# Layer 2: the last nine groups take all their chunks from GpSimd's gathers

## The chip, the core and the metric

The kernel runs on one core of one Trainium2 chip. The core has TensorE (PE, matrix products), VectorE (DVE), ScalarE (ACT) and GpSimd (POOL), each with an instruction stream of its own, and SyncE (SP), which issues DMAs. They wait for one another through semaphores. The metric is the time of one execution on the device in microseconds; lower is better.

## The reference

A graph network of two layers on 12,500 nodes with 128 features and 200,000 edges, sorted by destination:

```python
h = relu(layernorm(x))
w = edge_weight / max(segment_sum(edge_weight, dst), EPS)[dst]
feat = relu(h @ W_pool + b_pool)
neigh = segment_max(feat[src] * w[:, None], dst)
rst = h @ W1_self + neigh @ W1_neigh + b1
h1 = relu(rst / max(norm(rst), EPS))
neigh2 = segment_sum(h1[src] * w[:, None], dst) / max(deg, 1)
out = x + relu(h1 @ W2_self + neigh2 @ W2_neigh + b2)
```

Nearly all the time goes into `feat[src]` and `h1[src]`: for each of the 200,000 edges one row of 128 numbers is fetched from a table of nodes.

## The kernel before

The edges are cut into 391 groups (`NG`) of 512, the last one of 320. A group has four chunks (`j` = 0 to 3) of 128 edges. Layer 1 ends, and layer 2 begins, a little past the middle of the execution; only layer 2 (from line 1134) is of interest here.

Group `g` needs the rows of the table for its 512 sources in a buffer with edges on the partitions. The eight buffers are a ring, `ring[g % 8]`, so group `g` can be filled only after the product of group `g - 8` has read the buffer. A chunk is fetched in one of two ways:

- GpSimd gathers it with one indirect DMA (`gather`, line 513): 128 rows of 512 bytes from the table `h_d` in device memory, one to each partition. The gathers of group `i` are issued at loop step `i`, but GpSimd runs ahead as far as the ring lets it.
- VectorE or ScalarE copies it by columns. The table also lies turned in SBUF (`other_way`: features on partitions, nodes along the free dimension), so one node is one column. ScalarE copies one column per instruction (`one_by_one`, line 792; 128 instructions a chunk), VectorE two (`two_by_two`, line 799; 64 a chunk). Each column's place is a register, loaded sixteen at a time (`places_of`, line 743) from a list that SyncE fetches (`load`, line 738). The chunk stands turned when it is full; TensorE transposes it into PSUM (`turned`, line 1152) and ScalarE writes it back to the buffer (`back`, line 1155).

Which chunks go by columns is set by the class `Columns` (line 711). In layer 2 VectorE takes chunk 1 of every third group from group 17 on, ScalarE chunk 2 of every third or fourth (3.5 on average) from group 12 on. The planner puts a chunk's eight bursts of sixteen columns into the loop steps from `g - 6` on, the transposition into step `g - 2` and the turn back into step `g`. `takes(g)` says whether the group is in the plan; `gather` skips such a chunk.

The loop (line 1218) writes out the order of each engine by hand. A step `i` holds: the gathers of group `i`; on VectorE the placement weights `s` of group `i` (`weighted_places`, line 1164: two instructions, three buffers); node transforms that are due (`nodes2`, line 903); on TensorE the product of group `i - 1` (`window_product`, line 1173: a clearing matmul, line 1177, and eight passes, line 1179, that sum the weighted rows of the edges into 48 destination columns in PSUM, with three accumulators `pa`); on VectorE the addition of group `i - 2` into the sums (`window_add`, line 1181); and column copies in between on VectorE and ScalarE. Every engine works its stream in order: a product that waits for one chunk holds all later products.

The end of the plan is the argument `end` of `Columns`: groups below it can be taken.

Of the kernel before, what the change touches and what calls it, by code (L numbers as in the profile page):

```python
# [43 lines left out]
HIGH = 1.0e30  # L44
KEPT = 4
PAIR = 2


@with_exitstack
def gnn_kernel(ctx, tc, x, src, dst, ew, w_pool, b_pool, w1s, w1n, b1, w2s, w2n, b2, out):  # L50
# [20 lines left out]
    NG = GF + 1  # L71
# [62 lines left out]
    def buffer(g, wide):  # L134
        if not wide:
            return ring[g % RING]
        if WIDE <= g < WIDE + 3:
            k = g - WIDE
            return (work(f"f{k}").rearrange("p (q d) -> p q d", d=D) if k < 2 else ewT[:, 1])
        h = g if g < WIDE else g - 3  # L140
        if h < LESS:
            return ring[h % WIDE]
        return mid[(h - LESS) % MID] if h < LEAST else ring[(h - LEAST) % RING]
# [463 lines left out]
    for i in range(len(groups) + 4):  # L607
# [57 lines left out]
        while raw_chunks and 1 <= i <= 15:  # L665
            r, j = raw_chunks[0]
# [119 lines left out]
    def lists_of(k):  # L786
        return [listed[at:at + 1, :] for at in (64 * k, 64 * k + 32)]

    def by_scalar(out, in_, **scale):
        nc.scalar.activation(out, in_, AF.Copy, **scale)  # L790
# [23 lines left out]
    def wide1(t):  # L814
        return PAIR if t < HI - LATE else 1

# [107 lines left out]
    with tc.manual_schedule(), tc.tile_pool(name="ew", bufs=3) as wk, \  # L924
# [15 lines left out]
        for k, engine, copy, j, every, first in (  # L940
# [6 lines left out]
            def slot(g, k=k, rows_of_chunk=rows_of_chunk):  # L947
                return rows_of_chunk(g) if k else picked[:, bycol[0].place[g], :]
# [185 lines left out]
    with tc.manual_schedule(), tc.tile_pool(name="ew2", bufs=3) as wk, \  # L1134
# [10 lines left out]
        for k, engine, copy, j, every, first in (  # L1145
                (0, mybir.EngineType.DVE, two_by_two, 1, 3, 17),
                (1, mybir.EngineType.Activation, one_by_one, 2, 3.5, 12)):

            def slot(g, j=j):
                return buffer(g, False)[:, j, :]  # L1150

            def turned(g, _, k=k, slot=slot):
                nc.tensor.transpose(flip[:, k], slot(g), ident)  # L1153

            def back(g, _, k=k, slot=slot):
                by_scalar(slot(g), flip[:, k], **({} if k else {"scale": signs}))

            bycol.append(Columns(engine, copy, None, other_way, 1, lists_of(k), slot,
                                 ((-2, turned), (0, back)), 3, j, every, first, NG - 1))
            bycol[k].turned, bycol[k].back = turned, back  # L1160
        nc.vector.memset(agg2, 0.0)
        ss, pas, xrs = ({} for _ in range(3))
# [196 lines left out]
def build(inputs):  # L1359
    import numpy as np  # L1360
    import concourse.bacc as bacc

    nc = bacc.Bacc("TRN2", target_bir_lowering=False, num_devices=1)
    arrays, args = {}, []
    for name in _INS:
        a = np.ascontiguousarray(inputs[name])
        arrays[f"in_{name}"] = a
        args.append(nc.dram_tensor(f"in_{name}", a.shape, mybir.dt.from_np(a.dtype),
                                   kind="ExternalInput").ap())
    args.append(nc.dram_tensor("out", inputs["x"].shape, F32, kind="ExternalOutput").ap())  # L1370
    with tile.TileContext(nc) as tc:
        gnn_kernel(tc, *args)
    return nc, arrays
# [7 lines left out]
```

## Time and profile before

| what | us |
|---|---|
| median of 3 runs | 5087.21 |
| lowest and highest run | 5079.45, 5088.45 |
| profiled execution | 5084.55 |
| span of the profiled execution, first to last instruction | 5082.8 |
| PE, DVE, ACT, POOL busy | 2223.8, 3212.2, 3309.8, 2622.4 |

In rows of a timeline the first number is the start in microseconds from the beginning of the span, the second the time from the first start to the last end of the instructions that the row merges (`x8`: eight of them). Then come engine, line, operation, `out<-in` and shapes; the brackets give the idle time of the engine before the row and what ended it. `gt` is a buffer of the ring, `way` the turned table or the sums, `pa` an accumulator, `flip` the PSUM tile of the transpositions. "issue" means that nothing in the profile ended the wait, "remote" that it was something outside the profile. In the chain of waits a row is a start, a duration and what the time went to, along the work that ended last. In rows of groups a row gives the number of instructions, their busy time, the mean in nanoseconds, and the idle time before them.

### The profile page before, as it was taken

The page shows a single profiled execution, that of the slowest core. Times are in us where ns is not written, and L with a number is a line of the kernel's source. Part 1 is how long each engine was busy: PE and PEld are TensorE (multiplying, and loading weights), DVE is VectorE, ACT ScalarE, POOL GpSimd, SP SyncE. Part 2 cuts the span into 40 slices and gives each one's busy share as a digit, 9 for nine tenths or more (in the row PEclk, how much of TensorE's full clock was granted, in tenths as well). Part 3 has the DMA queues.
Part 4 walks back from the last instruction along what each step waited for, and adds up shares of the span by engine and source line. Part 5 has one row for each costly group of instructions (what it writes and reads, how often), then busy time and mean ns, then how long its engine had stood idle before and what let it go on. Part 6 is the DMA issues. An engine that isn't in the chain of part 4 may idle for free.

```text
span 5082.8 us, 71968 instructions
## 1 busy us (share of the span) xinstructions
PE 2223.8 (44%) x9504; PEld 1947.8 (38%) x9504; DVE 3212.2 (63%) x16738; ACT 3309.8 (65%) x25632; POOL 2622.4 (52%) x2784
## 2 busy tenths in 40 slices
PE   5554445444444444444433444343443334334344
PEld 3344444444444434343333444333333333333334
DVE  4667767676676667666645666565555555655655
ACT  3467767677777767667636666666666666666665
POOL 4454554555555555555554555545544454554453
PEclk6655555555555555555555555555555555555555
DMA  4322222222222222222211111111111111111111
GB/s 151 105 69 59 63 62 59 64 61 62 62 62 63 62 61 63 62 63 62 62 51 35 37 50 46 40 40 40 43 40 41 40 41 40 42 41 39 42 43 36
DMA packets 132987, 280.13 MB, mean 55 GB/s; under 512 B 49446, under 2 KB 58764, under 8 KB 132494
## 3 DMA queue, kind: packets, MB, share of 16 engines
q0 software_dynamic: 88544, 181.42, 14.2%
q1 hardware_dynamic: 43214, 93.11, 5.4%
q14 instruction: 414, 3.39, 0.2%
q8 instruction: 79, 1.29, 0.1%
q10 hardware_dynamic: 736, 0.92, 0.1%
HBM read 253.41 MB, written 21.87 MB: 54 GB/s over the span
## 4 chain that ended last, share of the span: by engine, by line
ACT 50%; issue 33%; POOL 6%; PE 3%; ACTq 3%; DVE 2%; another core or an unknown queue 2%; DMA 1%; DVEq 0%; POOLq 0%
ACT gt L790 35%; ACT gs L1037 8%; POOL gt L520 5%; ACTq L744 3%; ACT rows L1052 2%; PE pa L1179 1%; ACT w2T L790 1%; ACT way L987 1%; ACT locT L790 1%; ACT sq L871 1%; DMA gt<-h_d,srcT 1%; PE pf L624 0%; DVE gt L802 0%; DMA gt<-feat_d,srcT 0%
## 5 line engine op out<-in xcount | busy, mean ns | idle before, releaser
L790 ACT ACTIVATE gt<-way 128x1 f32 x21376 | 2355.0, 190 | 1429.0 <-issue 1379.9
L520 POOL DMA_INDIRECT gt<-h_d,srcT x1318 | 1247.7, 947 | 1202.1 <-PE pa L1179 653.0
L520 POOL DMA_INDIRECT gt<-feat_d,srcT x1192 | 1128.4, 947 | 955.7 <-ACT rows L1052 454.4
L802 DVE SCALAR_TENSOR_TENSOR gt<-b,way 128x2 f32<-128x2 f32 x8000 | 1191.5, 216 | 582.4 <-issue 444.6
L1179 PE MATMUL pa<-s,gt 128*128 128x24 f32 x3102 | 760.2, 390 | 1032.9 <-ACT gt L790 767.0
L1179 PEld LDWEIGHTS pa<-s,gt 128*128 128x128 f32 x3102 | 699.6, 326 | 1115.7 <-ACT gt L790 777.5
L1057 DVE TENSOR_TENSOR_SCAN pm<-kt,carry,pm 128x512 f32<-128x512 bf16 x389 | 498.2, 1281 | 326.1 <-PE pm L1042 261.6
L1042 PE MATMUL pm<-ident,gs 128*128 128x128 f32 x1499 | 405.0, 425 | 604.6 <-ACT gs L1037 559.9
L802 DVE SCALAR_TENSOR_TENSOR picked<-b,way 128x2 f32<-128x2 f32 x3840 | 545.1, 213 | 24.1 <-issue 23.0
L1042 PEld LDWEIGHTS pm<-ident,gs 128*128 128x128 f32 x1499 | 286.3, 224 | 648.3 <-ACT gs L1037 603.0
L1037 ACT ACTIVATE gs<-gt,ewT 128x128 f32<-128x128 f32 x1303 | 417.8, 390 | 47.9 <-issue 38.4
L1106 PEld LDWEIGHTS pn<-sel,rows 128*128 128x128 f32 x1564 | 363.2, 320 | 208.8 <-ACT way L892 97.7
L1106 PE MATMUL pn<-sel,rows 128*128 128x48 f32 x1564 | 362.2, 379 | 177.7 <-ACT way L892 89.3
L1182 DVE TENSOR_TENSOR way<-pa,way 128x48 f32 x391 | 78.9, 202 | 274.2 <-PE pa L1179 122.5
L1069 DVE TENSOR_SCALAR sel<-cols,lastT,invT 128x48 f32<-128x48 f32 x782 | 246.9, 316 | 5.2 <-remote 5.1
L1153 PE MATMUL flip<-ident,gt 128*128 128x128 f32 x233 | 98.5, 455 | 343.2 <-ACT gt L790 313.0
L1097 PE MATMUL pr<-ident,sc 128*128 128x128 f32 x782 | 241.3, 411 | 16.1 <-issue 7.4
L1080 DVE COPY sc<-pm 128x256 f32<-128x256 f32 x391 | 161.7, 414 | 87.9 <-remote 54.0
L1153 PEld LDWEIGHTS flip<-ident,gt 128*128 128x128 f32 x233 | 62.8, 287 | 351.8 <-ACT gt L790 321.2
L1083 DVE COPY_PREDICATED sc<-kt,pm 128x256 f32<-128x256 int16 x389 | 168.6, 433 | 17.8 <-DVE sel L1069 10.9
L1097 PEld LDWEIGHTS pr<-ident,sc 128*128 128x128 f32 x782 | 168.0, 224 | 17.7 <-issue 16.0
L520 POOL DMA_INDIRECT w2T<-feat_d,srcT x96 | 91.3, 951 | 136.4 <-DVE raw_off L543 56.4
(303 smaller groups left out, 2801.5 us busy)
## 6 DMA issues: line engine op xcount, KB each, us to landing
kt<-keep_d SPq DMA_DIRECT2D x97, 512.0 KB
gt<-h_d,srcT POOLq DMA_INDIRECT x1318
gt<-feat_d,srcT POOLq DMA_INDIRECT x1192
feat_d<-fr SPq DMA_DIRECT2D x24, 256.0 KB
xr<-in_x SPq DMA_DIRECT2D x24, 256.0 KB
out<-o SPq DMA_DIRECT2D x24, 256.0 KB
h_d<-h SPq DMA_DIRECT2D x47, 128.0 KB
listed<-at_d SPq DMA_DIRECT2D x359, 0.5 KB
```

The lines of the kernel that those rows point to most:

```text
L520: nc.gpsimd.indirect_dma_start(out=gt[:k, j, :], out_offset=None, in_=table_d[:, :], in_offset=bass.IndirectOffsetOnAxis(ap=srcT[:k, t, j, ...
L790: nc.scalar.activation(out, in_, AF.Copy, **scale)
L802: nc.vector.scalar_tensor_tensor(slot[:, r + e:r + e + 2], zero_high, columns_read[e], columns_read[e + 1].to_broadcast([P, 2]), op0=OP.su ...
L1037: nc.scalar.activation(gss[i][:k, j, :], gt[:k, j, :], AF.Copy, scale=ewT[:k, t, j, r:r + 1])
L1042: nc.tensor.transpose(pms[i - 1][:, j * P:j * P + k], gs[:k, j, :], ident[:k, :k])
L1057: nc.vector.tensor_tensor_scan(pm[:, :ne], kt[:, :ne], pm[:, :ne], carry, op0=OP.add, op1=OP.max)
L1069: nc.vector.tensor_scalar(part, cols[:k, 1, :], lastT[:k, t, j, r:r + 1], invT[:k, t, j, r:r + 1], op0=OP.is_equal, op1=OP.mult)
L1080: nc.vector.tensor_copy(sc[:, :ne // 2], two[:, :, 1])
L1083: nc.vector.copy_predicated(sc[:, :ne // 2], new[:, :, 1], two[:, :, 0])
L1097: nc.tensor.transpose(prs[g][:k, j, :], sc[:, j * P:j * P + k], ident)
L1106: nc.tensor.matmul(pas[g], rows[:k, j, :], sel[:k, j, :], start=j == 0, stop=j == len(chunks) - 1)
L1179: nc.tensor.matmul(pas[g][:, SHIFT[j]:SHIFT[j] + CW], gt[:k, j, :], s[:k, j, :], start=False, stop=j == 0)
```

## The change

The plan of both engines in layer 2 ends at group `NG - 9` = 382 rather than at `NG - 1` = 390. VectorE's chunks of groups 383, 386 and 389 and ScalarE's of groups 383 and 386 leave the plan, with their list loads, register loads, copies, transpositions and turns back. GpSimd gathers these five chunks. Layer 1 keeps its plan.

```diff
@@ -44,6 +44,7 @@
 HIGH = 1.0e30
 KEPT = 4
 PAIR = 2
+CATCH = 9
 
 
 @with_exitstack
@@ -1156,7 +1157,7 @@
                 by_scalar(slot(g), flip[:, k], **({} if k else {"scale": signs}))
 
             bycol.append(Columns(engine, copy, None, other_way, 1, lists_of(k), slot,
-                                 ((-2, turned), (0, back)), 3, j, every, first, NG - 1))
+                                 ((-2, turned), (0, back)), 3, j, every, first, NG - CATCH))
             bycol[k].turned, bycol[k].back = turned, back
         nc.vector.memset(agg2, 0.0)
         ss, pas, xrs = ({} for _ in range(3))
```

## The prediction

> **What bounds the kernel now.** I read the page first, then the chain of waits over the last 40 us, then the timelines of ScalarE, GpSimd and TensorE there, and last the opening of layer 2, the one place where gathers run with few column copies beside them.
>
> ```profile
> span 5082.8 us, 71968 instructions
> ...
> ACT 50%; issue 33%; POOL 6%; PE 3%; ACTq 3%; DVE 2%; another core or an unknown queue 2%; DMA 1%; DVEq 0%; POOLq 0%
> ```
>
> ScalarE and the issue time around it hold most of the chain over the whole span. The change touches only the end, so the end decides:
>
> ```profile
> 5052.71 1.07 ACT gt L790 x8
> 5053.79 0.04 issue
> 5053.83 1.48 PE pa L1179 x6
> ...
> 5061.74 0.28 PE flip L1153
> ...
> 5071.13 1.52 PE pa L1179 x6
> ```
>
> Until 5053.8 the chain runs on ScalarE's column copies; from there it is TensorE alone, product after product. The timeline of TensorE, with the groups counted back from the last product (the only one of 64 rows, group 390):
>
> ```profile
> 5004.86 1.90 PE L1179 MATMUL pa<-s,gt 128*128 128x24 f32 x8
> ...
> 5053.83 1.48 PE L1179 MATMUL pa<-s,gt 128*128 128x24 f32 x6 [7.74 <-ACT gt L790]
> ...
> 5055.88 1.90 PE L1179 MATMUL pa<-s,gt 128*128 128x24 f32 x8
> 5057.71 0.22 PE L1177 MATMUL pa<-nothing,ones_r 1*128 1x48 bf16 x1
> 5057.86 1.90 PE L1179 MATMUL pa<-s,gt 128*128 128x24 f32 x8
> ...
> 5071.06 1.59 PE L1179 MATMUL pa<-s,gt 64*128 64x24 f32 x6
> ```
>
> These are groups 376, 383 (its last six matmuls), 384, 385 and 390. Group 383 waits 7.74 us for ScalarE; then 384 to 389 run back to back, 1.98 us a product with the node transforms between, and 390 starts at 5071.06. The span ends 11.74 us later; that remainder (product, node transforms, stores) is not touched.
>
> ScalarE, which TensorE waited for:
>
> ```profile
> 5002.62 0.25 ACT L790 ACTIVATE gt<-flip 128x128 f32<-128x128 f32 x1
> ...
> 5043.40 0.20 ACT L790 ACTIVATE gt<-way 128x1 f32 x1 [0.50 <-issue]
> 5044.11 9.25 ACT L790 ACTIVATE gt<-way 128x1 f32 x92 [0.51 <-issue]
> 5053.27 0.35 ACT L790 ACTIVATE gt<-flip,b 128x128 f32<-128x128 f32 x1
> ```
>
> The copy at 5002.62 turns back group 376's chunk, and the sixteen copies before it were the last of group 379's. All single columns between 5002.86 and 5053.27 belong to groups 383 and 386. They go at two paces: 92 in 9.25 us, 0.1 us each, and one in 0.7 us (5043.40 to 5044.11). GpSimd's timeline tells them apart:
>
> ```profile
> 5005.15 0.95 POOL L520 DMA_INDIRECT gt<-h_d,srcT  x1 [0.30 <-PE pn L853]
> 5006.41 0.94 POOL L520 DMA_INDIRECT gt<-h_d,srcT  x1 [0.30 <-issue]
> 5009.13 0.95 POOL L520 DMA_INDIRECT gt<-h_d,srcT  x1 [1.78 <-remote]
> ...
> 5040.98 0.95 POOL L520 DMA_INDIRECT gt<-h_d,srcT  x1 [0.30 <-issue]
> 5045.95 0.95 POOL L520 DMA_INDIRECT gt<-h_d,srcT  x1 [4.02 <-issue]
> 5047.20 0.94 POOL L520 DMA_INDIRECT gt<-h_d,srcT  x1 [0.30 <-issue]
> ```
>
> The two at 5005 and 5006 are group 383's, 5009.13 opens group 384, 5040.98 ends 389, and 5045.95 opens 390's three, which end the queue. Gathers stand 1.25 us apart (5045.95, 5047.20). The slow pace of ScalarE ended at 5044.11, three microseconds after the run of gathers that ended at 5040.98. The three late gathers slowed nothing: the 92 copies ran through them. So a long run of gathers slows the other engines, and does so to their messages too: product 376 was through at 5006.76 by its row, and the gather that needs its buffer (376 and 384 share one of eight) started only at 5009.13. I call such a stretch a jam.
>
> **The change part by part.** Chunks 383, 386 and 389 of VectorE and 383 and 386 of ScalarE become gathers.
>
> Removed on ScalarE: 2 x 128 = 256 column copies. The groups between 5002 and 5054:
>
> ```profile
> L790 ACT ACTIVATE gt<-way 128x1 f32 x264 | 29.5, 190 | 21.3 <-issue 21.1
> L802 DVE SCALAR_TENSOR_TENSOR gt<-b,way 128x2 f32<-128x2 f32 x191 | 28.8, 216 | 13.7 <-issue 12.9 <-remote 0.4
> ```
>
> That is 29.5 us of work and 21.3 us of waiting beside it, nearly all of ScalarE's stretch up to 5053.27. ScalarE drops out of the tail; what is late next is either a gather or TensorE. On VectorE 3 x 64 = 192 instructions go, 28.8 us with 13.7 of idle. Those are covered today: 389's chunk is wanted only by a product after 5064, so I take 0 to 1 us for them, and count the gain that they let the weights of the next groups out sooner as nothing. Five list loads on SyncE and their register loads go too; nothing waits behind them at the end, 0. Five transposes and five turns back go; one transpose, 0.28 us in the chain at 5061.74, lies on the path that I keep, so 0.3 us is gained there.
>
> Added on GpSimd: five gathers, 5 x 1.25 = 6.25 us of its queue, two for 383, two for 386, one for 389. How they land: in the opening of layer 2 a product starts as the last gather of its group has landed,
>
> ```profile
> 2613.76 0.95 POOL L520 DMA_INDIRECT gt<-h_d,srcT  x1 [0.31 <-issue]
> ```
> ```profile
> 2608.55 1.90 PE L1179 MATMUL pa<-s,gt 128*128 128x24 f32 x8 [13.35 <-DVE place L1167]
> ...
> 2616.41 1.87 PE L1179 MATMUL pa<-s,gt 128*128 128x24 f32 x8 [2.97 <-DMA gt<-h_d,srcT]
> ...
> 2663.72 1.90 PE L1179 MATMUL pa<-s,gt 128*128 128x24 f32 x8
> ```
>
> so 2616.41 - 2613.76 = 2.65 us from a gather's start to its use.
>
> Now the replay. GpSimd: 383's four gathers run at 5005.15, 5006.41, 5007.66, 5008.91. The jam lasts as long after the run as before, so 384 follows after the same stop, 5009.13 - 5006.41 = 2.72 us, at 5011.63. Each later group waits for the product eight groups earlier. The trace does not show how many products get through in a jam without column copies. Between none and all, I take stops at 386 and 390: eight gathers (384, 385) from 5011.63 to 5020.38, stop, sixteen (386 to 389) from 5023.10 to 5041.85, stop, 390's three from 5044.57, the last at 5047.07, usable at 5049.72. One stop more or less is 2.72 - 1.25 = 1.5 us.
>
> TensorE: 390's first gather needs product 382 to be done and known. TensorE has three accumulators, so it can run at most two products beyond what VectorE could add; I take both, 383 and 384, as done by 5044.57, since nothing of ScalarE holds them any more. Left are 385 to 389, which took 5071.06 - 5057.86 = 13.20 us, less the 0.28 of the transpose. Product 390 starts at 5044.57 + 12.92 = 5057.49, well after its gathers. Against 5071.06 that is **13.6 us**. If only 382 is done, two products of 1.98 us come on top and 9.6 us remain; with one stop more, 8. With two products more and one stop less it is 19. These are the ends for this case.
>
> A rule against the jam: the Trainium skill, "SBUF — State Buffer", section "Who interferes with whom", says that a DMA never contends with a compute engine and that only the port pair shared by VectorE and GpSimd does. The rows here disagree for whatever reason: ScalarE's copies went from 0.1 to 0.7 us apart during the gathers. By the rule the new gathers would delay no engine, which is the third rival's price.
>
> **The rivals.** *The gathers eat it.* The stops of before stay as they are and the five gathers are only added: 390 opens at 5045.95 + 6.25 = 5052.20, product 382 is barely known then, and 383 to 389 follow in 13.20 + 2 x 1.98 = 17.16 us; 390 starts at 5069.4, a gain of 1.7 us, 5085.5 in the terms of the median. For it: GpSimd had stops that were not ScalarE's doing. Against it: the long idle before 5028 and 5045 went with groups that ScalarE and VectorE held.
>
> *The jam starves TensorE: slower.* With ever more gathers in a row the jam need not end. In the opening of layer 2, where gathers ran without a stop, products 3 to 9 took 2663.72 - 2608.55 = 55.17 us, 9.2 each, and VectorE stood still:
>
> ```profile
> 2630.26 0.21 DVE L1182 TENSOR_TENSOR way<-pa,way 128x48 f32 x1 [18.48 <-remote]
> ```
>
> At that pace products 376 to 382 end at 5004.86 + 7 x 9.2 = 5069.3, and 390 starts 17.16 us later, at 5086.4: 15.4 us slower, 5102.6. It decides from 7.0 us a product on ((5071.06 - 17.16 - 5004.86) / 7). Against it: at the opening GpSimd had eight empty buffers, and here each group waits for a product, which ends the run and lets the messages through.
>
> *TensorE keeps up.* With no column copies beside them the gathers slow nothing; 390 starts when its rows land, at 5049.72 with my stops (21.3 us gained, 5065.9), without any stop at 5005.15 + 30 x 1.25 + 2.65 = 5045.3 (25.8 us, 5061.4). For it: three gathers at 5045.95 slowed nothing. Against it: the opening, where VectorE had little to do and still stood for 18 us.
>
> **How the numbers follow.** The profiled execution took 5084.55 us, of which 5082.8 is the span; it lies 2.66 us below the median 5087.21. Less 13.6 it is 5071.0, in terms of the median 5073.6, rounded to 5074. Chances: forecast 0.55, gathers eat it 0.16, starved 0.12, keeps up 0.17. The forecast's own range is a gain of 8 to 19 us, 5068 to 5079. The range for the time reaches from inside the case that keeps up, 5064, to past the eaten one, 5086; outside are the starved case and the fastest end, together under 0.2. A measurement of this kernel tells about 0.2% from no change, 10.2 us. Of the forecast's 0.55 some 0.07 falls short of that. Faster: 0.48 + 0.17 = 0.65; within: 0.07 + 0.16 = 0.23; slower 0.12.
>
> **What would show it.** Right: no single-column copy of ScalarE after about 5003 (counted from the unchanged start of the tail, 80 us before the end); GpSimd in longer runs with stops of some 2.7 us; the first gather of 390 near 5044.6; TensorE's last product near 5057.5, with no wait for ScalarE among the last ten. The added gathers are right if they stand 1.25 us apart. Wrong: product 390 waiting for a gather (then TensorE keeps up), TensorE with waits of 5 us and more between products 376 and 382 (then it starves), or 390's gathers after 5050 (eaten). What would make it wrong above all is the number of products that pass in a jam, which I took as two beyond the last one known.

## The result, and the profile after

| kernel | median of runs, us | lowest, highest |
|---|---|---|
| before, 12 runs on the same chip | 5088.59 | 5079.45, 5097.99 |
| changed, 12 runs | 5083.87 | 5073.76, 5087.32 |
| ratio | 0.9985 | 0.9976 to 0.9994 |

The change gained 7.6 us by the ratio (0.15% of 5088.59; 3.1 to 12.2 by the interval), below the 0.2% that I called telling from no change. The ratio goes by all runs; the two medians lie only 4.7 us apart. The time lies within the stated range of 5064 to 5086, but the gain is just under the 8 us at which the forecast's own range began, and the forecast gain of 13.6 us lies just above the interval.

The tail can be measured more sharply than the total, since executions of one kernel already differ by up to 8 us when the tail begins. From the start of product 375, which the change does not reach, to the start of product 390:

| execution | 375 starts | 390 starts | tail, us |
|---|---|---|---|
| before, first profile | 5001.16 | 5071.06 | 69.9 |
| before, again (e5) | 5001.77 | 5071.24 | 69.5 |
| changed, first profile | 5000.29 | 5061.10 | 60.8 |
| changed, again (e6) | 5008.17 | 5069.00 | 60.8 |
| predicted | 5001.16 | 5057.49 | 56.3 |

The starts of product 375 in the two profiles of the kernel before and in e6 are these rows of TensorE's timeline; those of the changed kernel's first profile stand below.

```profile
5001.16 1.90 PE L1179 MATMUL pa<-s,gt 128*128 128x24 f32 x8
```
```profile
5001.77 1.90 PE L1179 MATMUL pa<-s,gt 128*128 128x24 f32 x8
```
```profile
5008.17 1.90 PE L1180 MATMUL pa<-s,gt 128*128 128x24 f32 x8
```

So 8.7 to 9.1 us came out of the tail, and 4.5 us of the forecast did not. Lines of the changed kernel stand one lower than before (L790 is L791, L1179 is L1180). Its page first, then its chain of waits, then the timeline of TensorE:

```profile
span 5073.8 us, 71452 instructions
...
ACT 51%; issue 31%; DVE 4%; ACTq 4%; PE 3%; POOL 3%; another core or an unknown queue 3%; DMA 1%; DVEq 0%; SPq 0%; POOLq 0%
...
L791 ACT ACTIVATE gt<-way 128x1 f32 x21120 | 2329.3, 191 | 1400.5 <-issue 1379.9
```
```profile
5018.88 5.91 another core or an unknown queue
...
5025.31 16.30 another core or an unknown queue
...
5042.13 7.30 another core or an unknown queue
5049.43 0.20 DVE way L1183
...
5050.15 1.90 PE pa L1180 x8
```
```profile
5000.29 1.90 PE L1180 MATMUL pa<-s,gt 128*128 128x24 f32 x8
...
5006.26 1.90 PE L1180 MATMUL pa<-s,gt 128*128 128x24 f32 x8
...
5017.58 1.90 PE L1180 MATMUL pa<-s,gt 128*128 128x24 f32 x8
...
5019.56 1.90 PE L1180 MATMUL pa<-s,gt 128*128 128x24 f32 x8
...
5025.53 1.90 PE L1180 MATMUL pa<-s,gt 128*128 128x24 f32 x8 [0.27 <-DVE s L1172]
...
5042.36 1.90 PE L1180 MATMUL pa<-s,gt 128*128 128x24 f32 x8 [0.28 <-DVE s L1172]
...
5050.15 1.90 PE L1180 MATMUL pa<-s,gt 128*128 128x24 f32 x8 [0.27 <-DVE s L1172]
...
5061.10 1.59 PE L1180 MATMUL pa<-s,gt 64*128 64x24 f32 x6
```

The products are 375, 377, 382, 383, 384, 385, 386 and 390. ScalarE is gone from the end of the chain, where "another core or an unknown queue" stands instead: a wait whose release the profile cannot name. Products 377 to 383 start 2.2 us apart. Then 384 to 386 take 30.6 us (5019.56 to 5050.15), 10.2 each, and 386 to 390 follow freely in 10.95. The timelines of GpSimd and VectorE show what stood there:

```profile
5008.05 0.94 POOL L521 DMA_INDIRECT gt<-h_d,srcT  x1 [0.30 <-issue]
5011.15 0.94 POOL L521 DMA_INDIRECT gt<-h_d,srcT  x1 [2.17 <-PE pa L1180]
...
5039.92 0.94 POOL L521 DMA_INDIRECT gt<-h_d,srcT  x1 [0.30 <-issue]
5041.87 0.94 POOL L521 DMA_INDIRECT gt<-h_d,srcT  x1 [1.01 <-remote]
...
5044.37 0.91 POOL L521 DMA_INDIRECT gt<-h_d,srcT  x1 [0.30 <-issue]
```
```profile
5024.81 0.21 DVE L1183 TENSOR_TENSOR way<-pa,way 128x48 f32 x1 [5.76 <-remote]
...
5041.63 0.21 DVE L1183 TENSOR_TENSOR way<-pa,way 128x48 f32 x1 [16.15 <-remote]
...
5049.42 0.21 DVE L1183 TENSOR_TENSOR way<-pa,way 128x48 f32 x1 [7.11 <-remote]
```

GpSimd issued all 24 gathers of 384 to 389 in one run, 1.25 us apart, and 390's three after a gap of 1.95. VectorE's three rows are the additions of products 381, 382 and 383, counted back from the last. Product 382 was through at 5017.58 + 1.90 = 5019.48, and VectorE could add it only at 5041.63, 22.2 us later; product 385 needs the accumulator that this addition frees.

The trace also records each update of a semaphore. A product posts five to TensorE's semaphore: one with the clearing matmul and one with every second pass. Those of the changed kernel from 5020 on, in us:

```
5020.53  5022.66  5024.78 | 5026.89  5029.01  5032.51  5036.71  5041.61 |
5045.11  5047.94  5048.65  5049.35  5049.40 | 5049.43  5049.47  5049.52 ...
```

At each bar the fifth update of a product is in, and VectorE's addition follows 0.02 to 0.03 us later (5024.81, 5041.63, 5049.42). The updates come out one at a time, at distances that are multiples of 0.70 to 0.71 us (2.12, 3.50, 4.20, 4.90), though TensorE finished all of 381 to 383 by 5021.5. After 5049.35 the rest comes out 0.04 us apart. So for TensorE the jam is a backlog of messages. ScalarE's single copies of before had the same distance (5043.40 to 5044.11), but the profile does not name what they waited for.

### The profile page after: what moved, and what is told of

It is laid out like the page before. It is cut to its first block, busy times and chain, and to the rows that moved or that the text cites. A ratio compares the mean times of both kernels' runs of the same rounds, so it can differ in the third digit from the quotient of the medians.

```text
span 5073.8 us, 71452 instructions
## 1 busy us (share of the span) xinstructions
PE 2221.2 (44%) x9499; PEld 1946.7 (38%) x9499; DVE 3185.5 (63%) x16546; ACT 3283.6 (65%) x25371; POOL 2627.5 (52%) x2789
## 4 chain that ended last, share of the span: by engine, by line
ACT 51%; issue 31%; DVE 4%; ACTq 4%; PE 3%; POOL 3%; another core or an unknown queue 3%; DMA 1%; DVEq 0%; SPq 0%; POOLq 0%
ACT gt L791 37%; ACT gs L1038 8%; ACTq L745 3%; POOL gt L521 3%; ACT rows L1053 2%; PE pa L1180 1%; DVE gt L803 1%; ACT way L988 1%; ACT w2T L791 1%; ACT locT L791 1%; ACT sq L872 1%; DMA gt<-feat_d,srcT 1%; DVE pm L1058 0%; ACT gt L957 0%
## 5 line engine op out<-in xcount | busy, mean ns | idle before, releaser
L791 ACT ACTIVATE gt<-way 128x1 f32 x21120 | 2329.3, 191 | 1400.5 <-issue 1379.9
L803 DVE SCALAR_TENSOR_TENSOR gt<-b,way 128x2 f32<-128x2 f32 x7808 | 1164.5, 217 | 571.4 <-issue 448.1
L1180 PE MATMUL pa<-s,gt 128*128 128x24 f32 x3102 | 759.1, 390 | 1012.4 <-ACT gt L791 770.8
L1180 PEld LDWEIGHTS pa<-s,gt 128*128 128x128 f32 x3102 | 699.0, 326 | 1112.3 <-ACT gt L791 780.8
L1084 DVE COPY_PREDICATED sc<-kt,pm 128x256 f32<-128x256 int16 x389 | 169.8, 437 | 13.6 <-DVE sel L1070 8.3
```

The costliest lines, as they stand in the source:

```text
L803: nc.vector.scalar_tensor_tensor(slot[:, r + e:r + e + 2], zero_high, columns_read[e], columns_read[e + 1].to_broadcast([P, 2]), op0=OP.su ...
L1084: nc.vector.copy_predicated(sc[:, :ne // 2], new[:, :, 1], two[:, :, 0])
L1180: nc.tensor.matmul(pas[g][:, SHIFT[j]:SHIFT[j] + CW], gt[:k, j, :], s[:k, j, :], start=False, stop=j == 0)
```

## The experiments

Twelve runs, on four chips. The chips turned out to be of two kinds: the kernel before takes about 5085 us where it was profiled first and on the chip of e5 to e8, and 3526 us on the three others (e1 to e4; e9 and e10; e11 and e12). No chip showed both. Each result is compared with the kernel before on its own chip. All edits are to the changed kernel; e5 is the kernel before, e6 and e10 are the changed kernel as it stands.

**e1 and e2: one engine's chunks alone.** Only ScalarE's two chunks become gathers, or only VectorE's three:

```diff
-                                 ((-2, turned), (0, back)), 3, j, every, first, NG - CATCH))
+                                 ((-2, turned), (0, back)), 3, j, every, first, NG - (CATCH if k else 1)))
```
```diff
-                                 ((-2, turned), (0, back)), 3, j, every, first, NG - CATCH))
+                                 ((-2, turned), (0, back)), 3, j, every, first, NG - (1 if k else CATCH)))
```

> Only ScalarE's two chunks (383, 386) become gathers; VectorE keeps 383, 386 and 389. Theory (ScalarE's copies were what the end waited for, and an unbroken run of gathers holds the other engines' messages): the wait of 7.7 us on ScalarE goes, two gathers instead of five are added, VectorE's 192 copies now end the tail at about the place where they ended before (5055), so the last product starts 3 to 9 us earlier than before: ratio to before 0.998 to 0.9995, no worse than the change. Rival (each of the five chunks is worth the same): two fifths of the change's gain, about 3 us, ratio 0.9994.

> Only VectorE's three chunks (383, 386, 389) become gathers; ScalarE keeps 383 and 386. Theory: ScalarE's copies still end at 5053 or, with three gathers more beside them, 1 to 4 us later; no gain, 0 to 4 us slower than before, ratio 1.000 to 1.0008, and TensorE's product of 383 still waits for ScalarE. Rival (each chunk worth the same): three fifths of the gain, about 4.5 us, ratio 0.9991.

Measured: e1 3526.15 against 3526.16, ratio 0.9999 (0.999 to 1.0008); e2 3517.45, ratio 0.9977 (0.9968 to 0.9986). On this chip it is VectorE's part that pays, the reverse of what I expected. The chain over the whole span says why (it stands at e10): there VectorE holds most of it, not ScalarE. TensorE in e1, and then in e2:

```profile
3497.58 1.91 PE L1180 MATMUL pa<-s,gt 128*128 128x24 f32 x8 [2.51 <-DVE s L1172]
...
3510.79 1.59 PE L1180 MATMUL pa<-s,gt 64*128 64x24 f32 x6
```
```profile
3484.41 1.47 PE L1180 MATMUL pa<-s,gt 128*128 128x24 f32 x6 [7.07 <-ACT gt L791]
...
3501.15 1.59 PE L1180 MATMUL pa<-s,gt 64*128 64x24 f32 x6
```

With VectorE's column copies left in, the placement weights `s` come late; with ScalarE's left in, a product still waits 7.07 us for them, and 390 nevertheless starts 9.6 us earlier than in e1. What each part is worth on the chip of the prediction these two runs do not say.

**e3, e9, e11: a stop before 387.** Groups 387 to 390 take the buffers of 383 to 386, so that GpSimd must wait for product 383:

```diff
-            return ring[g % RING]
+            return ring[(g - 4 if g >= NG - 4 else g) % RING]
```

> The changed kernel, with groups 387 to 390 put into the buffers of groups 383 to 386, so that GpSimd has to stop for a product four groups back. Theory (an unbroken run of gathers holds TensorE's and VectorE's messages; a stop lets them through): one to three stops in the run that now goes from 5011 to 5040, the last gather 2 to 6 us later, but at least three products more are done by then, so the last product starts 4 to 9 us earlier than in the changed kernel: ratio to before 0.9965 to 0.998. Rival (the engines' own work sets the pace and stops only cost time): 2 to 5 us slower than the changed kernel, ratio 0.999 to 0.9997.

> Groups 387 to 390 in the buffers of groups 383 to 386 once more, for a chip with slow stretches. Theory (messages of TensorE and VectorE are held while gathers run without a stop, and a stop lets them through): the run of 24 gathers is broken once, after group 386, products 384 to 386 follow during the stop and just after it, the last product starts 4 to 12 us earlier than in the changed kernel, ratio to before 0.9960 to 0.9980. Rival (a stop only costs time): 2 to 5 us later than in the changed kernel, ratio 0.999 to 0.9997. On a chip without slow stretches: 0.9975 again.

> Groups 387 to 390 in the buffers of groups 383 to 386, for a chip with slow stretches. Theory (messages of TensorE and VectorE are held while gathers run without a stop, and a stop lets them through): the run of 24 gathers is broken after group 386, the last product starts 4 to 12 us earlier than in the changed kernel, 49 to 57 us after product 375 instead of 60.8, ratio to before 0.9960 to 0.9980. Rival (a stop only costs time): 63 to 66 us after product 375, ratio 0.999 to 0.9997. On a chip without slow stretches: 0.9976 again.

Measured: ratios 0.9975 (0.9966 to 0.9984), 0.9976 (0.9965 to 0.9986) and 0.9977 (0.9968 to 0.9986); medians 3517.23, 3517.58 and 3518.62. All three fell on chips of the 3526 us kind, and there no stop came of the edit: in e3 product 383 is through at 3477.80, and 387's first gather follows the one before it after the usual 1.25 us:

```profile
3480.44 0.94 POOL L521 DMA_INDIRECT gt<-h_d,srcT  x1 [0.30 <-issue]
```

So these three runs are the change itself once more. They say nothing of a stop; whether one shortens a jam stays open.

**e4: no stop at all.** Groups 383 to 390 get eight buffers that layer 2 has free:

```diff
+    spare = [ewT[:, t] for t in range(NT)]
+    spare += [a[:, t:t + 2].rearrange("p t q n -> p (t q) n") for a in (lastT, invT) for t in (0, 2)]
...
-            return ring[g % RING]
+            return spare[g - NG + 8] if g >= NG - 8 else ring[g % RING]
```

> The changed kernel, with groups 383 to 390 in eight buffers of their own, so that no gather from 383 on waits for a product. Theory (an unbroken run holds the messages): about 35 gathers in one run, ending near 5043 as now, but TensorE has only about product 378 behind it then and twelve are left: the last product starts 8 to 14 us later than in the changed kernel, ratio to before 1.000 to 1.002. Rival (waits for buffers only cost time): 0 to 3 us faster than the changed kernel, ratio 0.998 to 0.9985.

Measured: 3515.66, ratio 0.9971 (0.996 to 0.9983), like the change itself on such a chip (e10). The slowdown that my theory wanted did not show, but it could not: in e10 the gathers from 381's first to the last run 1.25 us apart without this edit, so there was no stop to take away.

**e5 and e6: both kernels again, on a chip of the 5085 us kind.**

> The kernel before once more, for its profile beside the others. If the chip is as in the first four experiments (3526 us, no slow stretches beside gathers): VectorE's column copies end last in the tail, some 9 us after those of a kernel without them, and no gap of 0.7 us between ScalarE's copies while gathers run. If it is as in the first profile (5085 us): the tail of that profile again.

> The changed kernel beside the kernel before on one chip. Theory for a chip without slow stretches: VectorE's copies set the end before, and with all five chunks moved the gathers set it, so about what the kernels with other buffers gave: ratio 0.9965 to 0.9980 (7 to 12 us), TensorE's last products wait for gathers. Rival (the gain comes from the stops, as on the first chip): 0.9985 as measured at first. On a chip with slow stretches: 0.9976 to 0.9994 again.

Measured: e5 5084.67 (one run); e6 5078.18 against 5085.46, ratio 0.9987 (0.9978 to 0.9996). TensorE in e5, at products 383 and 390, and in e6, at 383 to 386 and 390:

```profile
5054.01 1.48 PE L1179 MATMUL pa<-s,gt 128*128 128x24 f32 x6 [9.22 <-ACT gt L790]
...
5071.24 1.59 PE L1179 MATMUL pa<-s,gt 64*128 64x24 f32 x6
```
```profile
5027.47 1.90 PE L1180 MATMUL pa<-s,gt 128*128 128x24 f32 x8
...
5036.16 1.91 PE L1180 MATMUL pa<-s,gt 128*128 128x24 f32 x8 [0.27 <-DVE s L1172]
...
5052.35 1.90 PE L1180 MATMUL pa<-s,gt 128*128 128x24 f32 x8 [0.28 <-issue]
...
5058.05 1.90 PE L1180 MATMUL pa<-s,gt 128*128 128x24 f32 x8 [0.27 <-DVE s L1172]
...
5069.00 1.59 PE L1180 MATMUL pa<-s,gt 64*128 64x24 f32 x6
```

The picture repeats: the same wait for ScalarE in the kernel before (9.22 us here), and in the changed kernel three products in 30.6 us (5027.47 to 5058.05), then 10.95 us to 390. The order of the stops differs a little (GpSimd stood 3.16 us before 390's gathers here), the sum does not.

**e7: the last gathers left out.** The kernel does not gather the chunks of groups 384 to 390; their products read what the buffers held:

```diff
-                gts[i] = gather(buffer(i, False), h_d, i, besides=bycol)
+                gts[i] = gather(buffer(i, False), h_d, i, besides=bycol) if i < NG - 7 else buffer(i, False)
```

> The changed kernel without the gathers of groups 384 to 390 (seven groups leave out fetching their rows and use what lies in the buffers). Theory: without these gathers TensorE's products follow at 1.98 us and nothing holds them: the last product starts 10 to 16 us earlier than in the changed kernel on a chip without slow stretches, 25 to 30 us earlier on one with them. Rival (TensorE's and VectorE's own work sets the end): less than 3 us earlier on either.

Measured: 5038.62 (one run). TensorE at products 375, 382, 383 and 390:

```profile
4988.60 1.90 PE L1180 MATMUL pa<-s,gt 128*128 128x24 f32 x8
...
5005.84 1.90 PE L1180 MATMUL pa<-s,gt 128*128 128x24 f32 x8
...
5007.82 1.90 PE L1180 MATMUL pa<-s,gt 128*128 128x24 f32 x8
...
5024.71 1.59 PE L1180 MATMUL pa<-s,gt 64*128 64x24 f32 x6
```

The tail is 36.1 us against 60.8 in e6 on the same chip, 24.7 less, just under the 25 to 30 that I expected. (The rest of the difference in the total lies ahead of the tail: this one execution reached product 375 19.6 us before e6's, and the edit does not touch what comes before.) Products 383 to 389 start every 1.98 us but for the node transforms, and TensorE's updates come about 0.43 us apart within a product, with no distance of 0.70. So neither TensorE's work nor VectorE's sets the 60.8, and the slow updates need the gathers beside them.

**e8: eight more buffers earlier.** The spare buffers of e4 go to groups 375 to 382, so that GpSimd is further ahead:

```diff
-            return ring[g % RING]
+            return (spare if NG - 16 <= g < NG - 8 else ring)[(g + 1) % RING]
```

> The changed kernel with eight further buffers for groups 375 to 382 (and the ring turned by one for the others), so that GpSimd can be up to sixteen groups ahead at the end. Theory (the end waits for gathers that start late): the gathers of the last groups start up to 10 us earlier, ratio to before 0.994 to 0.997, below that of the changed kernel. Rival (GpSimd's queue is full anyway, so that more buffers give nothing): as the changed kernel to 0.0005.

Measured: 5089.66 against 5085.46, ratio 1.0011 (1.0002 to 1.002): slower than before, and 11.5 us slower than e6 on the same chip, where I expected a gain. The profiled execution took 5081.64 us, one of the fastest of its eleven, so its total does not show the loss; its last 25 products do. From the start of product 366 to that of 390 they take 135.5 us (4931.72 to 5067.22) against 120.1 in e6 (4948.95 to 5069.00). TensorE (the second half of 368, then 375 and 390), GpSimd (the first and the last gather of its long run, and the last of all), and one of ScalarE's copies beside that run:

```profile
4989.54 1.05 PE L1183 MATMUL pa<-s,gt 128*128 128x24 f32 x4 [52.53 <-ACT gt L794]
...
5032.19 1.90 PE L1183 MATMUL pa<-s,ewT 128*128 128x24 f32 x8
...
5067.22 1.59 PE L1183 MATMUL pa<-s,gt 64*128 64x24 f32 x6
```
```profile
4931.63 0.94 POOL L524 DMA_INDIRECT gt<-h_d,srcT  x1 [7.00 <-PE pa L1183]
...
4979.08 0.94 POOL L524 DMA_INDIRECT gt<-h_d,srcT  x1 [0.30 <-issue]
...
5033.72 0.90 POOL L524 DMA_INDIRECT gt<-h_d,srcT  x1 [0.30 <-issue]
```
```profile
4959.19 0.20 ACT L794 ACTIVATE gt<-way 128x1 f32 x1 [1.20 <-issue]
```

GpSimd issues 39 gathers in one run. Beside it ScalarE's single copies stand mostly 1.4 us apart, twice the 0.70, and product 368 waits 52.53 us until ScalarE turns its chunk back; the changed kernel waits 16.59 there. So the products are kept back: 375, which the changed kernel starts at 5000.29, starts at 5032.19, and the sixteen products left then need 35.0 us, about TensorE's own pace (36.1 in e7). The gathers end 10.7 us earlier than the changed kernel's 5044.37, to no use. Letting GpSimd run further ahead makes the jam longer; what TensorE waits for here are ScalarE's column copies, which layer 2 still has before group 383, and not its own messages.

**e10: the change on a chip of the other kind**, and **e12: four buffers for the last eight groups**, which makes GpSimd wait long there:

```diff
-            return ring[g % RING]
+            return ring[(NG - 12 + (g - NG + 8) % 4 if g >= NG - 8 else g) % RING]
```

> The changed kernel beside the kernel with the stop, on the same chip. With slow stretches: 60 to 61 us from product 375 to product 390 again, ratio to before 0.998 to 0.9995. Without: 0.9965 to 0.998, the tail set by the gathers, which end near where they end in the kernel with the stop, as no gather there waits.

> Groups 383 to 390 share four buffers, so that every gather from 383 on waits for the product four groups back: a stop before 383 and more later. Theory with slow stretches: the stop before 383 costs about 8 us of the gathers' time, the later ones let the products through, the last product 55 to 61 us after product 375, no better than with the one stop. Rival (a stop only costs time): 68 us and more. Without slow stretches stops only cost time: 5 to 12 us slower than the changed kernel, ratio to before 0.9985 to 1.0010.

Measured: e10 3517.18 against 3526.3, ratio 0.9972 (0.9962 to 0.9982); e12 3528.15 against 3527.45, ratio 1.0004 (0.9995 to 1.0013). From e10 the page's chain and its group of column copies, then the timelines of TensorE (375, 387, 388, 390) and of GpSimd:

```profile
DVE 46%; ACT 18%; issue 11%; DMA 8%; POOL 7%; DVEq 5%; PE 5%; ACTq 1%; POOLq 0%; SPq 0%
...
L791 ACT ACTIVATE gt<-way 128x1 f32 x21120 | 2100.6, 189 | 223.6 <-PE pa L1180 159.6
```
```profile
3455.46 1.90 PE L1180 MATMUL pa<-s,gt 128*128 128x24 f32 x8
...
3485.28 1.87 PE L1180 MATMUL pa<-s,gt 128*128 128x24 f32 x8 [2.58 <-DMA gt<-h_d,srcT]
...
3490.33 1.87 PE L1180 MATMUL pa<-s,gt 128*128 128x24 f32 x8 [3.03 <-DMA gt<-h_d,srcT]
...
3499.16 1.59 PE L1180 MATMUL pa<-s,gt 64*128 64x24 f32 x6
```
```profile
3496.46 0.90 POOL L521 DMA_INDIRECT gt<-h_d,srcT  x1 [0.30 <-issue]
```

Here the products wait for the landing of their own gathers and 390 starts 2.70 us after the last one: the third rival, "TensorE keeps up", as written, with the tail at 43.7 us. TensorE's updates come about 0.43 us apart within a product (3465.45, 3465.87, 3466.30, 3466.73) beside gathers 1.25 us apart. VectorE holds 46% of the chain and ScalarE 18%, against 4% and 51% in the changed kernel's first profile. GpSimd in e12:

```profile
3472.73 0.94 POOL L521 DMA_INDIRECT gt<-h_d,srcT  x1 [10.19 <-PE pa L1178]
```

It is the only stop that the four buffers brought, and on such a chip it is all loss: some 11 us against the change by the two ratios, as expected there. The wait before ScalarE's column copies, 1400.5 us in the changed kernel's first profile, is 223.6 in e10. The difference of 1177 us is three quarters of the 1562 between the two spans (5073.8 and 3511.5): most of what parts the kinds of chip is waiting where columns are copied beside gathers, over the whole execution.

## Why the prediction was right or wrong

- **ScalarE leaves the path: right.** Its last column copy ends at 5001.8, and none of the last ten products waits for it. Product 383 starts at 5019.56, where before it waited until 5053.83, and that wait is gone in both profiles of the changed kernel. VectorE's chunks were put at 0 to 1 us; no run on this kind of chip moved one engine's chunks alone, so how the gain divides between the two is not shown.
- **Five gathers cost 6.25 us of the queue: right.** They stand 1.25 us apart. Group 384's first came at 5011.15 (predicted 5011.63).
- **Stops at 386 and 390: one of the two came.** Products 375 to 383 came through early in the run, so no buffer of 384 to 389 was late and 24 gathers went in one run, without the stop before 386. The stop before 390 came: its buffer is free after product 382, whose fifth update is in at 5041.61. 390's gathers opened at 5041.87 rather than 5044.57; 0.9 us of that is this execution's earlier tail, so they came 1.8 us sooner, which is not in the sum, since no product waited for them.
- **Two products beyond 382 done by 5044.57: one too few.** With three accumulators TensorE can run three products past the last one that VectorE has added, not two: 385 starts at 5042.36, after the addition of 382 at 5041.63, and 386 only after that of 383 at 5049.42. So 385 was done too (5042.36 + 1.90 = 5044.26), which leaves 10.95 us rather than 12.92 and saves 1.97.
- **385 to 389 following freely from 5044.57: the step that failed.** The sum lets them go as 390's gathers open and puts no wait behind that, because three late gathers had slowed nothing before. Here the backlog of messages lasted until 5049.4, 5.0 us after the start of the last gather of all, and product 386 started at 5050.15; in e6 it lasted 2.9 us past the last gather's start, although a stop had come before 390's. So a wait of the products after the gathers, which the sum has at nothing, was there both times. Moved by the 0.9 us, the prediction let the products go at 5043.70; they went 6.45 us later. Less the 1.97, an error of the other sign, that is the 4.5 us missed.
- **"Gathers eat it": excluded.** It wanted 390's gathers at 5052.20.
- **"The jam starves TensorE": its mechanism, without its price.** 384 to 386 went at 10.2 us each, past the 7.0 from which that rival decides and close to the 9.2 of layer 2's opening. But 377 to 383 were through before the jam told; the rival took the pace to hold from 376 on. e8 comes near to what the rival named, the gathers early, the products kept back, slower than before, but there TensorE waited for ScalarE's copies.
- **"TensorE keeps up": false on the chip of the prediction, true on the other kind.** The Trainium skill, "SBUF — State Buffer", section "Who interferes with whom", has the rule that was weighed there: a DMA never contends with a compute engine. Of the work itself the trace of the kernel before bears it out: ScalarE's 155 column copies between 5005 and 5043.9, in the jam, take 191 ns in the mean, and the 92 after it 188. What was held up in the tail of the changed kernel is TensorE's messages, which decided the time.

Shown: that the gathers make the slow tail (e7), that the late additions wait for updates that come out singly (the trace of the changed kernel, and the 0.43 us spacing of e7 and e10), and that a longer run ahead of the last column copies costs more than it gives (e8). Not shown: what occupies the slots of 0.70 us, why a backlog outlasts the start of the last gather by 2.9 us once and by 5.0 another time, and why some chips have none of it. Nor is it shown that messages are all that is held: at the opening of layer 2 in the kernel before, TensorE's single passes start at 2632.34, 2635.16, 2637.25 and 2640.06, multiples of 0.70 apart like ScalarE's copies, and the profile names nothing that they waited for. Fewer updates a product, one instead of five, would be the edit to try next; it was not tried. No version here beat both kernels by more than its interval: e2, e3, e4, e9 and e11 equal the change on their kind of chip, e12 loses the gain there, and e8 loses on the other.

## What to carry to other kernels

Where a wait ends with something that the profile cannot name, count the semaphore updates that it needs against the times at which they were recorded: a message can be late by 22 us, as here, when its work is long done. Giving an engine's copies to a queue of gathers can move the cost to whoever sends messages beside that queue, as on the first kind of chip here, and letting the gathers run further ahead can make it worse. A price found on one chip holds for its kind: here the part of the change that pays was another on the second kind.

## What the runs showed of the hardware that was not expected

- The changed kernel, at nearly the same granted clock (0.524 in its first profile, 0.539 in e10), spans 5073.8 us on one chip and 3511.5 on another, 44% more, with gathers 1.25 us apart in the runs of both.
- On the slower kind, semaphore updates beside a long run of gathers come out singly, at multiples of 0.70 to 0.71 us, and then in a burst 0.04 us apart.
- The delay grows along the run: in the changed kernel's first profile the fifth update of products 379 to 383 came 0.5, 2.8, 7.3, 22.1 and 27.9 us after the end of the product. In e7, without the gathers beside them, 380's came 0.02 us after it.
- A burst starts 2.7 to 2.9 us after the start of the last gather before it in four places (5008.05 to 5010.85 in the changed kernel's first profile, 5015.90 to 5018.75 and 5054.35 to 5057.26 in e6, 4996.38 to 4999.07 in e7). That is about what a gather takes from its start to its use (2.70 us in e10), so a backlog may last until the last rows have landed; at the end of the changed kernel's first profile it lasted 5.0 us, which does not fit.
